# Where an attention pair's step yields: before its masks, or behind its scores over global keys

## The chip, the cores and the metric

One core of one Trainium2 chip runs the whole program. Five engines work side by side, each through its own queue in order: PE (TensorE, matrix products, whose weight loads are listed as PEld), DVE (VectorE), ACT (ScalarE), POOL (GpSimd) and SP (SyncE, which here issues the transfers). The metric is the device time of one execution in microseconds; lower is better. Times of the kernel are medians over runs, and a profile is one execution taken by the hardware profiler.

## The reference

The program is a network of two blocks on x of shape (16, 512, 256): 16 sequences, 512 tokens, 256 channels. Each block adds a gated branch twice, after a layer norm with a modulation:

```python
h = _layernorm(x, axis=-1) * (1 + ca) + sa
x = x + ga * _L0_attn_ref(h, ...)      # recurrent "fast weights", chunks of 16 tokens
h = _layernorm(x, axis=-1) * (1 + cb) + sb
x = x + gb * _L0_ffn_ref(h, ...)       # low-rank: two products, Gelu, two products
...
x = x + ga * _L1_attn_ref(h, L1_attn_w_attn, L1_attn_w_proj)   # the part that is changed
...
x = x + gb * _L1_ffn_ref(h, ...)       # squared-relu channel mix with a sigmoid gate
```

The branch that the change touches is attention with 16 heads of 16 channels, over a window of 64 tokens and four global keys:

```python
i = np.arange(T)[:, None]
j = np.arange(T)[None, :]
causal = j <= i
local = causal & (j >= i - LOCAL_WINDOW + 1)
mask = local | g_row & causal | g_col & causal      # g_row, g_col: tokens 0 to 3
...
att = jnp.einsum('bhqd,bhkd->bhqk', q, k) * scale
att = jnp.where(mask, att, jnp.finfo(att.dtype).min)
att = jax.nn.softmax(att, axis=-1)
y = jnp.einsum('bhqk,bhkd->bhqd', att, v)
```

## The kernel before

**Units and streams.** The work is cut into 16 units u: half of the sequences (8 of 16) times 64 tokens, halves alternating. Each unit passes five streams, written as Python generators: `prepare` (projections, short convolution, spilled to DRAM), `chain` (the recurrence: two pieces of 32 tokens, each two chunks of 16; the two halves have separate chains that run at the same time), `mlp` (output projection of the recurrence, then the low-rank branch with its burst of eight Gelu), `attend` (the windowed attention) and `mix` (the channel mix). A stream runs up to its next `yield`, which is one step.

**What sets the order.** `timetable` (L1120) gives each step of a unit a due time by hand, for instance 24 for `attend`, the last 19 of them between u + 3.05 and u + 3.95; L1135 sorts all steps of all units by due time and writes them in that order. So instructions of one step stand together in program order, and between two steps of one stream stand steps of others. The tile framework then gives every instruction its place in its engine's queue when the kernel is built: of what it takes to be ready, the earliest written goes first (two bursts are raised by `high_priority`). Tiles with one tag share a fixed number of slots.

**PSUM.** Eight banks: one holds the recurrence's state (`fw`), three are shared by everybody under the tag `bank`, four under `abank`. An abank is asked for by `sc` (four at a time), `st` (four), `py` and `pz` (one each), and by `ph` of the Gelu burst.

**An attention pair.** `window_attention` (L769) treats the eight sequences of a unit as four pairs r. A pair has the steps

- `find_maxima(r)` (L877): scores `sc` with queries in rows, masks, a maximum on DVE (`mx`, L888); for far units (tb > 1) also scores `sg` over the global keys. POOL splits the maxima in three bf16 parts. It is run one pair ahead.
- `weigh(r)` (L904), first step: two dummy matmuls (`hold`, L194) and a transposition of the maxima into `pmx`, ACT copies it to `mxT` (L910), then scores `st` with keys in rows (L916) and the maxima subtracted by matmuls with `sel` (L920). The step ends there (L921).
- second step: four mask matmuls (L924, recorded at L869), four exponentials `pT` on ACT (L926); for far units scores `tg` over the global keys, two `hold` matmuls, the exponential `pg` (L938), and the global keys' part of `py` (values) and `pz` (sums); then the window's part of `py` (L957) and `pz` (L966). All products of `mm` are recorded at L872.
- third step: 1 / pz by Ln and Exp on ACT (`rs`, L976, L977), and `yT` on DVE (L981).

After each two pairs comes the projection `pproj` (L1003).

**Neighbours in the order.** Between the first and the second step of the pairs the due times put, in the middle of the kernel: a norm of `channel_mix` (transposes `pt_d`, L361, which eight ACT instructions `hp`, L367, read), its product `pka` (L1040, whose end ACT's `mix`, L1030, and `ka`, L1052, wait for), and `prepare`'s product `pp` (L441) with a norm `pt_c` of the next attention. The `ph` burst of a unit is written between the second and the third step of another unit's second pair. The recurrence's exponentials on ACT are L541 (`e_k`, `e_v`) and L612 (`hid`).

Of the kernel before, what the change touches and what calls it, by code (L numbers as in the profile page):

```python
# [95 lines left out]
def adaln_blocks(ctx: ExitStack, tc: tile.TileContext, a: dict, out: bass.AP):  # L96
# [14 lines left out]
    def bank(name):  # L111
        return ps.tile([P, 512], F32, tag="bank", name=name)

    def abank(name):
        return ps_a.tile([P, 512], F32, tag="abank", name=name)
# [4 lines left out]
    def t2k(stream, name, shape=None):  # L120
        return work.tile(shape or [P, 512], F32, tag=f"t2k_{stream}", name=name, bufs=RING[stream])
# [72 lines left out]
    def hold(dst, n):  # L194

        for _ in range(n):
            nc.tensor.matmul(
                dst, lhsT=ident, rhs=w_attn[:, 0, : dst.shape[1]], start=True, stop=True, skip_group_check=True
            )
# [569 lines left out]
    def window_attention(i, x):  # L769
# [4 lines left out]
        far, last = tb > 1, tb == T // TB - 1  # L774
# [88 lines left out]
        def window(r, k2, e):  # L863
            return keys[:, k2, r, 2 * e : 2 * e + 2].rearrange("p s t -> p (s t)")

        def add_mask(dst, query_first):
            at = 2 * min(tb, 2) + (0 if query_first else 6)
            m = masks[:, at : at + 2].unsqueeze(1).to_broadcast([P, 2, 2, P])
            nc.tensor.matmul(dst, lhsT=ident_bf, rhs=m, start=False, stop=True, skip_group_check=True)  # L869

        def mm(dst, lhsT, rhs, start=False):
            nc.tensor.matmul(dst, lhsT=lhsT, rhs=rhs, start=start, stop=False, skip_group_check=True)  # L872
# [31 lines left out]
        def weigh(r, outs):  # L904
            tag, q = f"{i}_{r}", queries(r)
            pt = bank(f"pmx{tag}")
            hold(pt[:, P:], 2)
            nc.tensor.matmul(pt[:, :P], lhsT=maxima[r % 2], rhs=ident_bf, start=True, stop=True)
            mxT = work.tile([P, P], BF16, tag="mxT", name=f"mxT{tag}", bufs=1)
            nc.scalar.copy(mxT, pt[:, :P])  # L910

            st = [abank(f"st{tag}_{j}") for j in range(4)]
            for s, k2, e in slots:
                for j in range(4):
                    rows = slice(32 * j, 32 * (j + 1))
                    mm(st[j][:, s * P : (s + 1) * P], window(r, k2, e)[rows], q(k2, e)[rows], s == 0)  # L916
            for s, k2, e in slots:
                for j in range(4):
                    rows = slice(32 * j, 32 * (j + 1))
                    mm(st[j][:, s * P : (s + 1) * P], sel[rows, s : s + 1].to_broadcast([32, P]), mxT[rows])  # L920
            yield  # L921
            pT = []
            for j in range(4):
                add_mask(st[j], False)  # L924
                pT.append(t2k("c", f"pT{tag}_{j}"))
                nc.scalar.activation(pT[j], st[j], AF.Exp)  # L926
            py, pz = abank(f"py{tag}"), abank(f"pz{tag}")
            if far:

                rg = slice(32 * r, 32 * (r + 1))  # L930
                tg = bank(f"tg{tag}")
                for s, k2, e in slots:
                    mm(tg[rg, e * P : (e + 1) * P], kglob[:, b0 + 2 * r + e, 16 * k2 : 16 * k2 + 32], q(k2, e), s == 0)
                for e in range(2):
                    mm(tg[rg, e * P : (e + 1) * P], selg[:, e], mxT)
                hold(tg[:, 2 * P :], 2)
                pg = work.tile([P, 2 * P], F32, tag="pg", name=f"pg{tag}", bufs=1)
                nc.scalar.activation(pg[rg], tg[rg, : 2 * P], AF.Exp)  # L938
                for s, k2, e in slots:
                    for j in range(4):  # L940
                        cols = slice(k2 * P + 32 * j, k2 * P + 32 * (j + 1))
                        mm(
                            py[32 * j : 32 * (j + 1), s * P : (s + 1) * P],
                            vglob[half][rg, e, cols],
                            pg[rg, e * P : (e + 1) * P],
                            s == 0,
                        )
                for k2 in range(2):
                    for j in range(4):
                        n = 4 * k2 + j  # L950
                        mm(
                            pz[32 * j : 32 * (j + 1), k2 * 2 * P : (k2 + 1) * 2 * P],
                            ones_g[rg, n : n + 1].to_broadcast([32, 32]),
                            pg[rg],
                            k2 == 0,
                        )
            for s, k2, e in slots:  # L957
                for j in range(4):
                    cols = slice(k2 * P + 32 * j, k2 * P + 32 * (j + 1))
                    mm(  # L960
                        py[32 * j : 32 * (j + 1), s * P : (s + 1) * P],
                        values[:, r, e, cols],
                        pT[j][:, s * P : (s + 1) * P],
                        s == 0 and not far,
                    )
            for s, k2, e in slots:  # L966
                for j in range(4):
                    mm(
                        pz[32 * j : 32 * (j + 1), s * P : (s + 1) * P],
                        ones,  # L970
                        pT[j][:, s * P : (s + 1) * P],
                        s == 0 and not far,
                    )
            yield
            rs = t2k("c", f"rs{tag}")
            nc.scalar.activation(rs, pz, AF.Ln)  # L976
            nc.scalar.activation(rs, rs, AF.Exp, scale=-1.0)  # L977
            yT = t2k("c", f"yT{tag}", [P, 2, 2, 2, WIN])
            halves = lambda t: t.rearrange("p (k e h t) -> p k e h t", k=2, e=2, h=2)
            for k2 in range(2):  # L980
                nc.vector.tensor_tensor(  # L981
                    yT[:, k2].rearrange("p h e t -> p e h t"), halves(py)[:, k2], halves(rs)[:, k2], mul
                )
            outs.append(yT)
# [4 lines left out]
        for b2 in range(NR // 2):  # L989
            gt = load_gate("c", 2, b0 + 4 * b2, f"c{i}_{b2}")  # L990
            outs = []
            for r in (2 * b2, 2 * b2 + 1):
                if r + 1 < NR:
                    find_maxima(r + 1)
                    yield
                yield from weigh(r, outs)
                yield
            po = bank(f"pproj{i}_{b2}")

            for n, yT in enumerate(outs):  # L1000
                for k2 in range(2):
                    for par in range(2):
                        nc.tensor.matmul(  # L1003
                            po[:, n * C : (n + 1) * C],
                            lhsT=yT[:, k2, par].rearrange("p e t -> p (e t)"),
                            rhs=w_proj[:, k2, par, :],
                            start=k2 == 0 and par == 0,
                            stop=k2 == 1 and par == 1,
                        )
            gated_residual("c", x, b2, po, gt, f"c{i}_{b2}")  # L1010
            yield
# [181 lines left out]
```

## Time and profile before

| | |
|---|---|
| time, median of 3 runs | 3243.3 us (3237.48 to 3245.96) |
| the profiled execution | 3245.84 us, its span 3244.0 us |
| granted TensorE clock, mean | 0.823 |
| busy in 1250 to 1400 us, of 150 | PE 130.92, DVE 126.50, ACT 89.52, POOL 88.48 |
| busy in 2920 to 3244 us, of 324 | PE 282.29, DVE 79.00, ACT 144.21, POOL 73.92 |
| longest waits of ACT | xp for pp 142.4, e_k for DVE 136.9, e_v for DVE 120.4, rs for pz 115.4 us |
| table loads on ACT | 103 at L224, 79 at L234, 15 at L541, 14 at L976, 10 at L977; 1283 ns each |

Busy time is the time in which an engine had an instruction running. The profile names a group of instructions by its line, engine and tiles (`py<-pT,values` is a product that writes py and reads pT and values). "31.1 <-ACT pT L926 30.2" behind such a group says that the engine stood idle for 31.1 us just before these instructions, and that 30.2 us of it ended when ACT's instruction at L926 finished. The chain of waits goes back from the last instruction, at each step to what released it; its shares say where the time lies that could not overlap. From about 2920 us on the recurrence has ended and only the last units' streams run.

### The profile page before, as it was taken

The numbers are of one execution on the slowest core, as the hardware profiler recorded it, in microseconds if no ns is written. First come the engines' busy times: TensorE is split into PE (matmuls) and PEld (weight loads), VectorE is DVE, ScalarE is ACT, GpSimd is POOL, SyncE is SP. The second block draws the span as 40 slices with busy tenths as digits, with TensorE's granted clock in tenths as the row PEclk, the third lists the DMA queues.
The fourth block names the chain that finished last, engine by engine and source line by source line (L and its number), as shares of the span: only waits on it lengthen the run. The fifth ranks groups of instructions, "written<-read, shape, count | busy, mean of one in ns | idle before, by whom it ended". The sixth has DMA issues, their size and how long they took to land.

```text
span 3244.0 us, 47232 instructions
## 1 busy us (share of the span) xinstructions
PE 2445.9 (75%) x17232; PEld 1472.7 (45%) x17232; DVE 2372.1 (73%) x4513; ACT 1762.4 (54%) x3738; POOL 1677.1 (52%) x1575
## 2 busy tenths in 40 slices
PE   3541156778787778988888888988888888889996
PEld 2110124444444445555455555554545555556564
DVE  1678787878868878878888888878878877873221
ACT  1652354555664656665665656565665545454543
POOL 0245555556656655655646565655556556553112
PEclk8775577878877887988889797989889787879898
DMA  5331112131403223130413122231404121112010
GB/s 150 75 69 20 46 34 70 31 73 39 97 17 77 62 57 76 48 85 21 103 30 94 45 68 65 51 83 34 99 14 105 28 70 37 57 39 59 17 28 27
DMA packets 439307, 186.46 MB, mean 57 GB/s; under 512 B 323937, under 2 KB 413090, under 8 KB 439074
## 3 DMA queue, kind: packets, MB, share of 16 engines
q1 hardware_dynamic: 439074, 183.44, 23.4%
q8 instruction: 135, 2.21, 0.3%
q14 instruction: 98, 0.80, 0.1%
HBM read 116.66 MB, written 66.72 MB: 57 GB/s over the span
## 4 chain that ended last, share of the span: by engine, by line
DVE 35%; POOL 22%; PE 21%; ACT 10%; issue 8%; DMA 3%; SPq 1%; POOLq 0%; DVEq 0%; ACTq 0%
POOL pd_o L533 6%; POOL pd_i L533 5%; DVE pd_kv L630 3%; DVE sc_v L526 3%; DVE pp L459 3%; DVE sv L527 3%; DVE mx L888 2%; DVE do L635 2%; PE st L872 2%; DVE di L635 2%; POOL pd_kv L533 2%; DVE scs L527 2%; PE pQ L742 1%; PE ph L735 1%; PE py L872 1%
## 5 line engine op out<-in xcount | busy, mean ns | idle before, releaser
L533 POOL TENSOR_TENSOR pd_o<-e_k,dt_v 128x1024 f32<-128x1024 f32 x128 | 299.4, 2346 | 242.0 <-DVE e_k L548 242.0
L533 POOL TENSOR_TENSOR pd_i<-e_v,dt_k 128x1024 f32<-128x1024 f32 x128 | 297.3, 2358 | 30.7 <-DVE e_v L548 30.7
L660 POOL TENSOR_TENSOR pd_kv<-hid,pd_kv 128x1024 f32<-128x1024 f32 x64 | 150.5, 2351 | 175.3 <-DVE fw L631 149.3
L872 PE MATMUL st<-qs,keys 32*128 32x128 f32 x2048 | 203.4, 321 | 46.2 <-DVE yT L981 23.3
L635 DVE TENSOR_REDUCE di<-pd_i 128x64 f32<-128x1024 f32 x128 | 155.6, 1216 | 108.6 <-POOL pd_i L533 108.6
L872 PEld LDWEIGHTS st<-qs,keys 32*128 32x128 f32 x2048 | 168.6, 211 | 122.0 <-DVE yT L981 34.3
L872 PE MATMUL sc<-keys,qs 32*128 32x128 f32 x2048 | 167.3, 327 | 74.1 <-DVE yT L981 47.9
L635 DVE TENSOR_REDUCE do<-pd_o 128x64 f32<-128x1024 f32 x126 | 152.9, 1215 | 91.2 <-POOL pd_o L533 91.2
L707 PE MATMUL pwo<-w_WoT,oT 128*128 128x256 f32 x256 | 107.0, 579 | 136.7 <-POOL oT L700 135.9
L872 PEld LDWEIGHTS sc<-keys,qs 32*128 32x128 f32 x2048 | 133.3, 215 | 141.0 <-DVE yT L981 51.2
L888 DVE TENSOR_REDUCE mx<-sc 128x4 f32<-128x512 f32 x256 | 168.0, 682 | 18.5 <-PE sc L869 18.3
L526 DVE TENSOR_TENSOR sc_k<-tok,fw 128x1024 f32<-128x1024 f32 x128 | 155.7, 1216 | 13.8 <-ACT tok L596 12.1
L533 POOL TENSOR_TENSOR pd_kv<-hid,dt_v 128x1024 f32<-128x1024 f32 x64 | 150.5, 2352 | 25.7 <-DVE hid L622 22.7
L630 DVE TENSOR_TENSOR_SCAN pd_kv<-within,pd_kv 128x1024 f32<-128x1024 bf16 x64 | 156.4, 2443 | 0.7
L526 DVE TENSOR_TENSOR sc_v<-tok,fw 128x1024 f32<-128x1024 f32 x128 | 151.0, 1216 | 1.5
L527 DVE TENSOR_REDUCE sv<-sc_v 128x64 f32<-128x1024 f32 x128 | 150.4, 1212 | 0.0
L981 DVE TENSOR_TENSOR yT<-py,rs 128x256 f32<-128x256 f32 x128 | 51.6, 417 | 131.2 <-ACT rs L977 130.8
L735 PE MATMUL ph<-PT,w_v 64*128 64x512 f32 x256 | 119.7, 725 | 34.9 <-ACT z L224 19.8
L707 PEld LDWEIGHTS pwo<-w_WoT,oT 128*128 128x128 f32 x256 | 69.3, 289 | 163.1 <-POOL oT L700 150.3
L1003 PE MATMUL pproj<-w_proj,yT 128*128 128x256 f32 x512 | 129.8, 395 | 17.1 <-DVE yT L981 12.6
L926 ACT ACTIVATE pT<-st 128x512 f32<-128x512 f32 x256 | 133.6, 619 | 15.7 <-PE st L869 15.6
L454 ACT COPY xp<-pp 128x512 f32<-128x512 f32 x96 | 56.6, 589 | 156.8 <-PE pp L441 142.4
(248 smaller groups left out, 7039.2 us busy)
## 6 DMA issues: line engine op xcount, KB each, us to landing
values<-values SPq DMA_DIRECT2D x56, 256.0 KB
gate_a<-gates SPq DMA_DIRECT2D x64, 128.0 KB
xa<-in_x_dram SPq DMA_DIRECT2D x32, 256.0 KB
x<-in_x_dram SPq DMA_DIRECT2D x32, 256.0 KB
gate_c<-gates SPq DMA_DIRECT2D x64, 128.0 KB
gate_d<-gates SPq DMA_DIRECT2D x64, 128.0 KB
q<-y SPq DMA_DIRECT2D x64, 128.0 KB
dt_q<-q SPq DMA_DIRECT2D x32, 256.0 KB
```

The costliest lines, as they stand in the source:

```text
L526: engine.tensor_tensor(pr, tok.unsqueeze(1).to_broadcast(every), w.unsqueeze(2).to_broadcast(every), mul)
L527: nc.vector.tensor_reduce(dst, pr, AX.X, add)
L533: engine.tensor_tensor(pr, hid.unsqueeze(2).to_broadcast(every), tok.unsqueeze(1).to_broadcast(every), mul)
L630: nc.vector.tensor_tensor_scan(flat, within, flat, 0.0, mul, add)
L635: nc.vector.tensor_reduce(t, pr, AX.X, add)
L660: nc.gpsimd.tensor_tensor(po, qh.unsqueeze(2).to_broadcast([P, R, D, CH]), upto, mul)
L707: nc.tensor.matmul(po[:, n * C : (n + 1) * C], lhsT=pair(oT, k, 2 * b2 + n), rhs=w_o[:, k, :], start=k == 0, stop=k == 1,)
L735: nc.tensor.matmul(ph, lhsT=w_v1[rows, f // 2, :], rhs=pT[rows], start=True, stop=True)
L872: nc.tensor.matmul(dst, lhsT=lhsT, rhs=rhs, start=start, stop=False, skip_group_check=True)
L888: nc.vector.tensor_reduce(mx[:, j], sc[j].rearrange("p (s k) -> p s k", s=NS), AX.X, ALU.max)
L926: nc.scalar.activation(pT[j], st[j], AF.Exp)
L1003: nc.tensor.matmul(po[:, n * C : (n + 1) * C], lhsT=yT[:, k2, par].rearrange("p e t -> p (e t)"), rhs=w_proj[:, k2, par, :], start=k2 == 0 ...
```

## The change

The `yield` between the first and the second step of `weigh` moves down: from behind the subtraction of the maxima to behind the exponential `pg` of the scores over the global keys (for near units, behind the four `pT`). The first step now ends with all exponentials written, and the second has the products with values and ones alone; the tiles `py` and `pz` are asked for behind the yield. The number of steps and all due times stay, and so does every instruction.

```diff
@@ -918,13 +918,11 @@
                 for j in range(4):
                     rows = slice(32 * j, 32 * (j + 1))
                     mm(st[j][:, s * P : (s + 1) * P], sel[rows, s : s + 1].to_broadcast([32, P]), mxT[rows])
-            yield
             pT = []
             for j in range(4):
                 add_mask(st[j], False)
                 pT.append(t2k("c", f"pT{tag}_{j}"))
                 nc.scalar.activation(pT[j], st[j], AF.Exp)
-            py, pz = abank(f"py{tag}"), abank(f"pz{tag}")
             if far:
 
                 rg = slice(32 * r, 32 * (r + 1))
@@ -936,6 +934,9 @@
                 hold(tg[:, 2 * P :], 2)
                 pg = work.tile([P, 2 * P], F32, tag="pg", name=f"pg{tag}", bufs=1)
                 nc.scalar.activation(pg[rg], tg[rg, : 2 * P], AF.Exp)
+            yield
+            py, pz = abank(f"py{tag}"), abank(f"pz{tag}")
+            if far:
                 for s, k2, e in slots:
                     for j in range(4):
                         cols = slice(k2 * P + 32 * j, k2 * P + 32 * (j + 1))
```

## The prediction

> **What bounds the kernel now.** I read the page's busy table first, then its chain, then the groups of the one pair step, then the order of time around two such steps.
>
> ```profile
> PE 2445.9 (75%) x17232; PEld 1472.7 (45%) x17232; DVE 2372.1 (73%) x4513; ACT 1762.4 (54%) x3738; POOL 1677.1 (52%) x1575
> PEclk8775577878877887988889797989889787879898
> DVE 35%; POOL 22%; PE 21%; ACT 10%; issue 8%; DMA 3%; SPq 1%; POOLq 0%; DVEq 0%; ACTq 0%
> ```
>
> No engine is full. The chain that ended last is the recurrence's for more than half (DVE 35%, POOL 22%); PE has 21% of it. In the windows view of 1250 to 2750 DVE is busy 120 to 126 of every 150 us, PE 124 to 130. Which of the two paces the middle? The copies to PT (L725, one for each unit) start at 1482, 1666, 1847, 2028, 2209 and 2391 us: a unit takes 181 to 184 us, although the granted clock of these windows moves between 0.84 and 0.91. So the middle hardly follows PE's speed. The last 324 us are different: there PE is busy 282.29, DVE 79.00, and the chain's largest lines are PE's.
>
> Now the step that is changed. The groups view gives what its matmuls waited for:
>
> ```profile
> L926 ACT ACTIVATE pT<-st 128x512 f32<-128x512 f32 x256 | 133.6, 619 | 15.7 <-PE st L869 15.6
> L872 PE MATMUL py<-pT,values 128*32 128x128 f32 x2048 | 110.5, 322 | 31.1 <-ACT pT L926 30.2
> L872 PE MATMUL py<-pg,vglob 32*32 32x128 f32 x1536 | 55.1, 283 | 38.7 <-ACT pg L938 38.7
> ```
>
> Over the kernel PE stands 30.2 + 38.7 = 68.9 us between its scores and its values, because the exponentials come between them. That is all that this change can take from PE. Two pair steps of one unit, in order of time (start, duration, engine, line; in brackets the idle time before it and who ended it):
>
> ```profile
> 1448.59 0.66 PE L361 MATMUL pt_d<-blocks,xn_d 128*128 128x128 f32 x4
> 1449.08 1.03 PE L869 MATMUL st<-masks,ident_bf 128*128 128x512 bf16 x4
> 1449.28 2.48 ACT L367 ACTIVATE hp<-pt_d,mod 128x64 f32<-128x64 f32 x8 [1.83 <-PE pt_d L361]
> 1451.61 2.10 ACT L926 ACTIVATE pT<-st 128x512 f32<-128x512 f32 x4
> 1453.93 1.44 PE L872 MATMUL py<-pg,vglob 32*32 32x128 f32 x32 [1.66 <-ACT pg L938]
> ...
> 1486.48 3.70 PE L1040 MATMUL pka<-mix,w_W_kT 128*128 128x512 f32 x8
> 1490.02 1.03 PE L869 MATMUL st<-masks,ident_bf 128*128 128x512 bf16 x4
> 1490.22 1.33 ACT L1030 ACTIVATE mix<-hp,mu 128x512 f32<-128x512 f32 x2 [5.24 <-PE pka L1040]
> 1491.46 2.04 ACT L926 ACTIVATE pT<-st 128x512 f32<-128x512 f32 x4
> 1493.95 1.07 PE L872 MATMUL py<-pg,vglob 32*32 32x128 f32 x32 [0.74 <-ACT pg L938]
> ```
>
> The other streams' work (pt_d, pka) stands before the masks, where nothing has to be waited for, and behind the masks PE waits. The four pairs of a unit have these waits before py: 1.66 (pt_d ahead of the masks), 0.74 (pka ahead), 0.46 (nothing of others near), 0.18 us (pp and pt_c); 3.04 together, and they repeat almost to the hundredth from unit 5 to unit 10.
>
> **The change part by part.** No instruction, transfer or wait is added or removed. The four masks, the four pT exponentials, and in a far unit tg's scores, its two hold matmuls and the pg exponential are written one step earlier, ahead of what other streams write between the two steps. The moved part issues nothing on DVE, POOL or SP and no DMA, so those queues keep their own order; what it is moved past on PE and ACT is pt_d/hp, pka/mix, pp and pt_c/hTc. abanks are asked for in the same order as before (st four, py and pz, then ph), and ph started right behind pz's first matmuls in every far unit, so I expect the ph burst to stay there.
>
> First, the waits. First pair: the masks come at pt_d's old place, 1448.6; the masks and tg take 3.2 us of PE (1449.08 to 1452.27), so they end at 1451.8; pT is no longer behind hp (2.48 us) and ends near 1451.1, pg near 1452.2, while PE does pt_d (0.66). The 1.66 goes. Second: pka (3.70) covers the exponentials; 0.74 goes. Third: nothing stands there to be put between; 0.46 stays. Fourth: pp covers; 0.18 goes. So 2.58 of 3.04 us, 85%; of 68.9 us that is 58 us of PE time.
>
> Second, what of it is on the path. Around 1448 the chain runs through POOL pd_o, DVE do and off_b, not through PE: the first pair's wait is hidden behind the recurrence there, and costs only where that cover is gone, in the tail. Around 1486 it runs through pka, mix, pT, pg, py, ph: the second pair's wait is on it. Second pairs from the first unit on wait 0.07, 1.04, 1.04, 1.05, nine times 0.74, then 1.71 and 1.79: 3.2 + 6.7 + 3.5 = 13.4 us. In the tail unit 14's first pair waits 4.02 us, and there the chain does go through hp and pT (2.36 and 1.95 us from 3011.07); I take 4.0. Gain: 17.4 us. The bounds are 7 us (the waits in the tail alone: pg 8.5 us from 2920 on, 85% of it) and 68.9 us (all).
>
> Third, what it costs. pt_d and pka start 3.2 us later, and their readers with them: hp, mix, ka. In the second pair ACT is without a gap from 1490.22 to the table load at 1496.95 that opens the Gelu burst. With pT and pg done by 1490.2, mix waits for pka until 1493.4 and ends at 1494.7, where mix, pT and pg together ended at 1493.9: the burst opens 0.8 us later, if the tok copies behind it stay behind it; 0 if they go first. I take 0.4, for 16 units 6 us (0 to 13). hp, 3 us later in the first pair, is followed by steps that wait long anyway (mixture, pka a unit's fifth later); nothing in the middle, at most 3 us where the tail has no cover. tg takes one of the three banks 3 us before pt_d or pka do, and gives it back as much earlier; nothing.
>
> Sum: 3245.84 (the profiled execution: span 3244.0 and 1.8 around it) - 17.4 + 6 = 3234.4. The median of the runs shown is 2.5 us below that execution, so 3232 in its terms, 0.35% faster.
>
> The clock I leave where it is. The row: from 1495.50 to 1502.30 the granted clock is 0.50 while PE is busy in all 6.80 us, and 1.00 in the 13.70 us before, with 12.96 busy. The Trainium skill ("TensorE: Matmul & The Clock Gate", What's actually happening) says that half rate follows an idle window of about 3.4 us and full rate a busy one; by it no wait of 0.2 to 1.7 us costs clock, and closing them brings none, so the sum stays. The row does not obey it cleanly, so the clock is an open term of either sign, which the unit lengths above bound: 3 us in 181 at most between 0.84 and 0.91.
>
> A rule against the change: the same page (Architectural detail: the array is 16× 32×32) says that ACT is a strict FIFO while PE may pull weight loads ahead. This trace agrees in kind: ACT stood 5.24 us at mix. By it, each of the delayed readers would hold up all of ACT, which is the second rival.
>
> **The rivals.** One: the waits go, and the time doesn't (or the order on PE comes out as it was). For it: the unit length that ignores the clock, and 22% of the chain on POOL; against it: the chain through the second pair. Time 3243, or 3236 if the tail's 7 us are kept.
>
> Two, slower: ACT's queue. Three of a unit's four pairs put ACT work of others (hp, mix, xp or hTc) behind PE work that now starts 3.2 us later. If such an instruction stands in ACT ahead of an exponential of the recurrence (e_k, e_v L541, hid L612), DVE and then POOL start late, and that chain is 57% of the path. One such meeting for each unit is 16 x 3.2 = 51 us; two halves alternate, so I count half: 26 us, time 3269. It decides once DVE's waits for these exponentials, now 18.8 + 5.8 + 20.4 = 45 us, pass some 60, since the gain is only 11. For it: ACT is 54% busy and in order, and the wait of ACT for pka is 76.2 us already. Against it: total ACT work is unchanged, and pT and pg move out of the same queue's later part.
>
> **How the numbers follow.** Forecast (waits go, partly on the path): 0.50, its own range 3205 to 3243. Hidden or not done: 0.12. Slower by ACT's queue: 0.38, from 3250 to 3295 (51 us, all of it, at the end). A change under 0.3%, 10 us, is what a measurement here can't tell from none. The forecast gives 0.42 faster and 0.08 same, the first rival 0.11 same and 0.01 faster, the second 0.37 slower and 0.01 same: 0.43, 0.20, 0.37. For 8 in 10 the range leaves out the gains over 43 us, which need waits removed that are hidden now, and the upper end of the second rival: 3200 to 3285.
>
> **What would show it.** Right: PE's idle time before py falls from 68.9 to about 10 us; between the last sel and the masks PE has no other stream's work, and pt_d, pka and pp stand between the hold matmuls and py; pT starts ahead of hp; the unit length stays 180 to 182. Wrong: py still waits on pg; ph enters before pz, or the burst's table loads (103 + 79 + 15 + 14 + 10) change in number; the wait of ACT for pka grows past 76.2 by more than 16 us; DVE's waits for e_k, e_v and hid pass 60; or the unit length moves by over 2 us, which would say that the order of the recurrence itself was changed by what was thought to be beside it.

## The result: 2.9% slower

The changed kernel takes 3339.27 us (median of 4 runs, 3338.53 to 3340.08), the kernel before beside it 3240.77 (4 runs): ratio 1.0292, 95% interval 1.0279 to 1.0306, 98.5 us more. The prediction, 3232 us in a range of 3200 to 3285, was wrong. These lines of the changed kernel's profile answer to those shown of the kernel before: the busy table, the granted clock in 40 slices, the chain by engine.

```profile
PE 2432.6 (73%) x17232; PEld 1492.8 (45%) x17232; DVE 2386.1 (71%) x4513; ACT 1771.8 (53%) x3738; POOL 1673.6 (50%) x1575
PEclk8775676878787879778888788888878887879998
PE 26%; DVE 19%; POOL 10%; ACT 7%; issue 5%; DMA 1%; SPq 0%; POOLq 0%; ACTq 0%; DVEq 0%
```

PE, DVE, ACT and POOL are busy for as long as before, within 15 us. So nothing was added; they wait more. The chain of the changed kernel is followed back to 1064 us only, so its shares add up to 68% and can't be laid beside those of before as they stand. Counted for both from 1502 to 2295 us, PE has 41% of it (21% before), DVE 29% (37%) and POOL 12% (23%): PE is ahead in the middle, where the recurrence was. The groups that changed (line, engine, tiles, count; busy us, mean ns; idle before them and who ended it):

```profile
L925 ACT ACTIVATE pT<-st 128x512 f32<-128x512 f32 x256 | 134.3, 603 | 88.6 <-PE st L869 88.6
L872 PE MATMUL py<-pT,values 128*32 128x128 f32 x2048 | 99.5, 311 | 18.4 <-ACT pT L925 17.7
L872 PE MATMUL py<-pg,vglob 32*32 32x128 f32 x1536 | 59.1, 297 | 29.4 <-ACT pg L936 29.1
L454 ACT COPY xp<-pp 128x512 f32<-128x512 f32 x96 | 56.4, 587 | 197.6 <-PE pp L441 183.5
L982 DVE TENSOR_TENSOR yT<-py,rs 128x256 f32<-128x256 f32 x128 | 50.5, 414 | 146.3 <-ACT rs L978 146.3
```

PE's wait ahead of py, which was to fall from 68.9 to about 10 us, is 17.7 + 29.1 = 46.8 us. pT stands early in ACT's queue, as foreseen, and there ACT waits for pT's masks: 88.6 us where it was 15.7. ACT's wait at xp, the entry of `prepare`, rose from 142.4 to 183.5 us.

The copies to PT, one for each unit, show where the time lies. Before they start at 1302, 1482, 1666, 1847, 2028, 2209, 2391 us, after at 1292, 1502, 1701, 1899, 2097, 2295, 2493. Until 1292 us the changed kernel is 10 us ahead; then one unit takes 210 us, and each that follows 198 in place of 181. The tail is as long as before (from the last PT 206 against 213 us). So the loss is in the far units of the middle, and it repeats.

One piece of a middle unit, in order of time (start, duration, engine, line; in brackets the wait):

```profile
1922.33 1.28 ACT L977 ACT_TABLE_LOAD   x1
1923.63 0.60 ACT L977 ACTIVATE rs<-pz 128x512 f32<-128x512 f32 x1
1924.24 1.28 ACT L224 ACT_TABLE_LOAD   x1
...
1928.90 1.09 ACT L224 ACTIVATE sg<-pr 128x512 f32<-128x512 f32 x2
1930.00 1.28 ACT L234 ACT_TABLE_LOAD   x1
1931.30 0.63 ACT L978 ACTIVATE rs<-rs 128x512 f32<-128x512 f32 x1
...
1931.96 0.76 DVE L982 TENSOR_TENSOR yT<-py,rs 128x256 f32<-128x256 f32 x2 [9.68 <-ACT rs L978]
```

The same instructions in the kernel before:

```profile
1869.56 0.60 ACT L976 ACTIVATE rs<-pz 128x512 f32<-128x512 f32 x1
...
1871.46 0.63 ACT L977 ACTIVATE rs<-rs 128x512 f32<-128x512 f32 x1
...
1872.13 0.76 DVE L981 TENSOR_TENSOR yT<-py,rs 128x256 f32<-128x256 f32 x2 [2.49 <-ACT rs L977]
```

The second pair's root, Ln and then Exp, stood within 1.9 us before, and DVE waited 2.49 us for it. Now the end of the Gelu burst and a Tanh burst with their table loads stand between the two, 7.7 us from start to start, and DVE, which has the recurrence behind it in its queue, stands for 9.68 us. Nothing in the change touches these instructions.

Over three middle units (from the eighth PT to the eleventh) DVE idles 31.0 us a unit before and 45.8 after, 14.8 of the 17 us. The two waits of DVE that grew most are this one at yT and one at `pp`, in `prepare`, for ACT's instruction on the same tile (0.6 us a unit before). In one unit, the first line before (1847.3 to 2028.2 us), the other two after (1899.3 to 2097.2; in all, times, longest):

```profile
DVE yT L981 <- ACT rs L977: 2.5, 1, 2.5
```

```profile
DVE yT L982 <- ACT rs L978: 9.9, 2, 9.7
DVE pp L459 <- ACT pp L457: 7.9, 2, 4.8
```

These two rose by as much as DVE's whole idle time; of the others some rose and some fell. At yT the lines above show the reason, ACT's new order. The wait at pp was not followed further.

### The profile page after: what moved, and what is told of

It reads as the page before. It is cut to its first block, busy times and chain, and to the rows that moved or that the text cites. A ratio compares the mean times of both kernels' runs of the same rounds, so it can differ in the third digit from the quotient of the medians.

```text
span 3337.4 us, 47259 instructions
## 1 busy us (share of the span) xinstructions
PE 2432.6 (73%) x17232; PEld 1492.8 (45%) x17232; DVE 2386.1 (71%) x4513; ACT 1771.8 (53%) x3738; POOL 1673.6 (50%) x1575
## 4 chain that ended last, share of the span: by engine, by line
PE 26%; DVE 19%; POOL 10%; ACT 7%; issue 5%; DMA 1%; SPq 0%; POOLq 0%; ACTq 0%; DVEq 0%
POOL pd_i L533 3%; DVE sv L527 2%; DVE sc_v L526 2%; PE st L872 2%; DVE pd_kv L630 2%; PE pQ L742 2%; PE ph L735 2%; PE pp L441 2%; PE pr L1061 2%; POOL pd_o L533 2%; PE pproj L1004 1%; PE pka L1041 1%; DVE pp L459 1%; PE sc L872 1%; PE pkv L1078 1%
## 5 line engine op out<-in xcount | busy, mean ns | idle before, releaser
L872 PE MATMUL sc<-keys,qs 32*128 32x128 f32 x2048 | 185.6, 321 | 80.3 <-DVE mx L888 73.9
L872 PEld LDWEIGHTS st<-qs,keys 32*128 32x128 f32 x2048 | 176.9, 223 | 126.3 <-DVE mx L888 47.0
L872 PEld LDWEIGHTS sc<-keys,qs 32*128 32x128 f32 x2048 | 155.4, 214 | 135.4 <-DVE mx L888 88.3
L707 PE MATMUL pwo<-w_WoT,oT 128*128 128x256 f32 x256 | 99.4, 553 | 149.6 <-POOL oT L700 134.2
L925 ACT ACTIVATE pT<-st 128x512 f32<-128x512 f32 x256 | 134.3, 603 | 88.6 <-PE st L869 88.6
L630 DVE TENSOR_TENSOR_SCAN pd_kv<-within,pd_kv 128x1024 f32<-128x1024 bf16 x64 | 174.7, 2730 | 0.6
L454 ACT COPY xp<-pp 128x512 f32<-128x512 f32 x96 | 56.4, 587 | 197.6 <-PE pp L441 183.5
L982 DVE TENSOR_TENSOR yT<-py,rs 128x256 f32<-128x256 f32 x128 | 50.5, 414 | 146.3 <-ACT rs L978 146.3
L1004 PE MATMUL pproj<-w_proj,yT 128*128 128x256 f32 x512 | 122.7, 386 | 12.5 <-DVE yT L982 10.5
```

The lines of the kernel that those rows point to most:

```text
L630: nc.vector.tensor_tensor_scan(flat, within, flat, 0.0, mul, add)
L707: nc.tensor.matmul(po[:, n * C : (n + 1) * C], lhsT=pair(oT, k, 2 * b2 + n), rhs=w_o[:, k, :], start=k == 0, stop=k == 1,)
L1004: nc.tensor.matmul(po[:, n * C : (n + 1) * C], lhsT=yT[:, k2, par].rearrange("p e t -> p (e t)"), rhs=w_proj[:, k2, par, :], start=k2 == 0 ...
```

## The experiments

Five theories were told apart. A: the root's two halves were parted. B: tg asks for one of three shared banks a step earlier. C: the moved work itself holds up PE's and ACT's queues. D: the order of all engines, made when the kernel is built, came out anew, and the new one is worse. E: PE's longer waits cost twice, by the clock that falls behind them. All times stand against runs of the kernel before on the same chip. "Unit" is the mean of three PT distances in the middle; "moved rows" counts, from the traces, the fewest of the 4513 rows of DVE's queue that must move to turn the order of the kernel before into that of the run (rows with the same tiles and shape are taken in order).

| run | time, us | ratio (95% interval) | unit, us | moved rows of DVE |
|---|---|---|---|---|
| before | 3243.3 | | 181 | |
| after | 3339.27 | 1.0292 (1.0279 to 1.0306) | 198 | 1148 |
| e1 second pairs alone | 3263.95 | 1.0076 (1.0061 to 1.0091) | 184 | 705 |
| e2 all but second pairs | 3332.19 | 1.029 (1.0272 to 1.0309) | 195 | 1049 |
| e3 masks and pT alone | 3282.65 | 1.0138 (1.0119 to 1.0157) | 188 | 1139 |
| e4 after, root raised | 3297.25 | 1.0184 (1.0165 to 1.0203) | 188 | 1276 |
| e5 before, root raised | 3247.4 | 1.0004 (0.999 to 1.0017) | 181 | 448 |
| e6 bank request alone | 3243.41 | 0.9995 (0.9986 to 1.0004) | 181 | 0 |
| e7 first pairs alone | 3324.47 | 1.0236 (1.0206 to 1.0267) | 197 | 936 |
| e8 fourth pairs alone | 3340.56 | 1.0287 (1.0264 to 1.0309) | 194 | 1085 |
| e9 49 pairs, queues held | 3284.43 | 1.0124 (1.0107 to 1.0141) | 188 | 0 |
| e10 same pairs, order free | 3310.87 | 1.0201 (1.0182 to 1.0219) | 194 | 1075 |
| e11 after, DVE and POOL as before | 3298.44 | 1.0168 (1.0153 to 1.0183) | 191 | 0 |
| e12 before, DVE and POOL as after | 3469.78 | 1.069 (1.0672 to 1.0708) | 209 | 1148 |
| e13 as e9, pT ahead of mix | 3270.38 | 1.0075 (1.0062 to 1.0088) | 184 | 0 |
| e14 after, waits filled | 3459.09 | 1.0656 (1.0643 to 1.067) | 201 | 1148 |
| e15 as e13, second pairs alone | 3242.38 | 0.9996 (0.9987 to 1.0005) | 181 | 0 |
| e16 as e13, first pairs alone | 3261.61 | 1.005 (1.0036 to 1.0063) | 183 | 0 |
| e17 due times shifted | 3279.21 | 1.0108 (1.0092 to 1.0123) | 186 | 886 |
| e18 after, waits filled less | 3339.47 | 1.0292 (1.0279 to 1.0306) | 198 | 1148 |

No version beats the kernel before.

### Parts of the change, order free: e1 to e4

e1 and e2 divide the change by pairs; the yield stands at its new place for some pairs and at the old for the rest. This is e1; e2 has `r != 1` in both conditions:

```diff
-            yield
+            if not (r == 1):
+                yield
...
+            if r == 1:
+                yield
             py, pz = abank(f"py{tag}"), abank(f"pz{tag}")
```

e3 puts the yield between the pT exponentials and `py, pz`, so that tg, its hold matmuls and pg stay behind it. e4 is the changed kernel with this edit:

```diff
-            nc.scalar.activation(rs, pz, AF.Ln)
-            nc.scalar.activation(rs, rs, AF.Exp, scale=-1.0)
+            with tc.high_priority():
+                nc.scalar.activation(rs, pz, AF.Ln)
+                nc.scalar.activation(rs, rs, AF.Exp, scale=-1.0)
```

> The yield stands at its new place for a unit's second pair (r == 1) alone, at the old one for the other three. Theory A (the roots parted): in the changed kernel the second pair's Ln of pz stands in the Gelu burst and its Exp behind that burst and the Tanh burst, 7.1 us after it, and DVE stands 9.7 us at yT in place of 2.5; 7.2 us for each of the six units that are 17 us longer, 43 us of the 98.5 lost. In this kernel's order the Exp is behind one Gelu and a table load, with no Tanh burst, so A expects yT's wait near 3 to 5 us, and 3240 to 3275 us. Theory B (the bank): tg asks for one of the three shared banks one step earlier, so pka or pp wait for it; here only pka is behind tg, so B expects a third of the loss, 3260 to 3280. Theory C (the other pairs do it: hp, pp and hTc behind pT in ACT's queue): near 3241.

> The other way round: new place for the first, third and fourth pair, old place for the second. A: in the middle units the second pair's Exp is only one copy behind its Ln, DVE does not stand at yT for long (under 3 us), so 3240 to 3290: what is left is what A does not explain. B: tg is ahead of pt_d, pp and pt_c, two thirds of the loss or more, 3305 to 3339. C: all of it, 3325 to 3340.

> Masks and pT are ahead of the yield in all four pairs, tg's scores, the hold matmuls and pg behind it with the values, so tg asks for its bank where it did before. B: the loss goes, 3235 to 3265. A: in this order the second pair's Exp stands behind five Gelu and two table loads, though not behind the Tanh burst, so yT still waits for some 6 to 8 us and 3290 to 3330. C: pT is as early as in the changed kernel, 3320 to 3340.

> The changed kernel with Ln and Exp of the roots (L976, L977 of before) raised to the front by the planner's priority, in all pairs: the second pair's Exp is then behind one Gelu and two table loads. A: yT's wait falls from 9.7 to some 3 to 5 us, and the time to 3270 to 3300 if only the direct 43 us come back, to 3240 if the rest followed from it. B and C: nothing of theirs is touched, 3325 to 3345.

Measured: 23, 92, 42 and 57 us slower than before. By the bounds that were set, e1 agrees with A and B, e2 with B and C, e3 with none of the three. The parts do not add: 23 and 92 make 115, and the whole is 98.5. e4 won back 42 us, as much as theory A asked for, and in its middle units DVE no longer waits at yT for ACT's root (0.0 us a unit in place of 9.9, the unit 188 in place of 198), while the wait at pp stays (8.8). But its order of DVE also differs from the changed kernel's in 925 rows, so that some of the 42 may be due to these. That left a loss which no single place held.

### Root and bank in the kernel before, single pairs: e5 to e8

e5 is e4's edit in the kernel before. e6 moves one line there, `tg = bank(f"tg{tag}")`, ahead of the old yield. e7 and e8 are e1's edit with `r == 0` and `r == 3`.

> The kernel before (all values behind the old yield), with only the two activations of the softmax's root (Ln and Exp to rs) raised in the order that is made at build. Nothing is left out. Theory A (in the changed kernel the loss of about 42 us comes from a root whose two halves were parted by the Gelu burst): before, the two halves stand 1.3 us apart, so nothing is to be mended; DVE waits only 2.5 us a unit at yT. By A the time is 3215 to 3245 (at best 16 x 1.7 us gained, at worst nothing). If raising the root is good by itself, whatever the place of the scores, e4's 42 us was no repair of the change's own damage and this run gains as much: about 3200.

> The kernel before, with only the request of tg's bank moved ahead of the yield; its matmuls, the masks and both exponentials stay behind it. Nothing is left out. Theory B (the three shared banks are handed out in the order of the requests, and tg asks one step earlier, ahead of pt_d, pka and pp, so a bank is held across the step and others' matmuls wait): the loss that went with tg's place (57 us, e3 against the change) appears here without any work moved, 3270 to 3300. Theory C (what costs is work: exponentials and matmuls ahead of other streams' in PE's and ACT's queues): no work has moved, 3241 within 10.

> The change for the first pair of each unit alone (pt_d/hp stand between its scores and values). Nothing is left out. The prediction: nothing in the middle, 3 to 4 us gained in the tail: 3237 to 3244. Theory B: one of three pairs with work of others behind tg, about a third of 57 us: 3255 to 3265. Theory C: hp behind pT and pg in ACT's queue, 3 us later for 16 units: up to 48 us, 3250 to 3290. Theory A has no part here (its root is the second pair's): the wait at yT stays at 2.5 us a unit.

> The change for the fourth pair of each unit alone (pp, pt_c, hTc stand between its scores and values). Nothing is left out. The prediction: 0.18 us a unit of wait goes, 3241 within 5. Theory B: tg's bank comes ahead of pp, which is the mixer's own input path (xp): a third to a half of 57 us, 3260 to 3275, with PE waiting at pp or pt_c for a bank. Theory C: xp and hTc late in ACT's queue, ACT's wait at xp for pp grows from 11.7 us a unit towards 20; 3250 to 3290. If pairs 0 and 3 each add up to little, the loss of e2 (91 us) is no sum over pairs.

e5 is the kernel before to 0.04%, so a raised root is no gain by itself. In e6 the build gave every engine the very order of the kernel before, so it says nothing against a bank that is held longer; it shows that the request's place remade nothing and cost nothing. e7 and e8 ended the sum by pairs: one pair in four costs 79 us, another 95, alone nearly what all four do together. No theory of a price at each place expects that.

What these slow kernels have in common is the last column of the table. The change issues nothing on DVE, and 1148 of DVE's 4513 rows stand elsewhere; of POOL's 1575 it is 339. Where no row moved (e6), no time moved. The count is no measure of the loss, though: in e5 448 rows moved and no time did, and e4 has more moved rows than the changed kernel and is faster.

### Queues held: e9 to e13, e15 and e16

The next kernels are built twice. The first build, of the kernel before, only gives its queues; in the second they are imposed by edges that order instructions without a wait:

```diff
+    for queue in order or []:
+        queue = [by_key[k] for k in queue]
+        for one, two in zip(queue, queue[1:]):
+            tc.add_manual_dep(
+                two, one.name, mybir.DependencyInfo(mybir.DependencyClass.NoSync, mybir.DependencyReason.DATA), reason="order"
+            )
```

In the traces of e9, e11, e13, e15 and e16 no row of DVE's or POOL's queue has another place than in the kernel before, and e15, as fast as that kernel, suggests that the edges by themselves cost nothing that can be seen. In e9 just the change's own instructions are then moved (PE's directly behind the last `sel` matmul, ACT's pT and pg ahead of the readers of what they passed):

```diff
+        pe[:] = rest[: a + 1] + mine + rest[a + 1 :]
...
+        hit = [n for n in range(max(0, p - 40), p) if reads(at[act[n]]) & late]
```

This could be done for 49 of the 64 pairs; for the other 15, nine of them the fourth pairs of units 4 to 12, the yield stays at its old place. That held queues and early scores would wait for each other there is not shown by a run.

> Every engine's queue is held in the order of the kernel before (DVE, POOL and SP to the last instruction), and only the change's own instructions are moved in PE's and ACT's queues: masks, tg's scores and hold matmuls directly behind the last sel matmul, pT and pg ahead of the readers of the work that they passed. That is what the prediction took the change to be. 49 of the 64 pairs are moved (all third pairs, 14 of 16 first ones, 12 second ones, 7 fourth ones); the other 15 stay as before. Nothing is left out. Theory D (the order of all engines is made anew at the build when one yield moves, and the loss is in the new order): the loss is gone, 3222 to 3245. Theory C (the moved work itself holds up PE's and ACT's queues): a large part of the loss stays, 3280 or more.

> The same 49 pairs divided at the new place as in e9, but the order of all engines left to the build. Nothing is left out. Theory D: as slow as the change, 3300 to 3345, so that the difference to e9 is the new order alone. If it comes out near 3241, the 15 pairs left out were the harmful ones, and e9 says nothing on the order.

> The change in full (64 pairs), with DVE's and POOL's queues held in the order of the kernel before; PE's, ACT's and SP's orders are left to the build. Nothing is left out. Theory D in its narrow form (the recurrence's order on DVE and POOL is what was lost): 3230 to 3260. If the new order of PE and ACT is what costs, or the moved work, it stays above 3290.

> The reverse: the program of the kernel before (old yield), with DVE's and POOL's queues held in the order that the changed kernel has; PE's, ACT's and SP's orders are left to the build. Nothing is left out. Theory D in its narrow form: the change's slowness comes without the change, 3300 to 3345. If the order of DVE and POOL is a mere consequence, 3241 within 20.

e9 was to decide between C and D. At 39 us slower it misses D's bound (3222 to 3245) and lies just inside C's (3280 or more), though most of the 98.5 us are gone. As its queues are those of the kernel before but for the moved instructions, its trace can be laid beside it instruction by instruction. The plainest difference is at one place of each unit, here in order of time:

```profile
1671.74 1.13 PE L197 MATMUL tg<-w_w_attnT,blocks 128*128 128x256 f32 x4
...
1672.71 3.60 PE L1046 MATMUL pka<-mix,w_W_kT 128*128 128x512 f32 x8
...
1676.35 1.33 ACT L1036 ACTIVATE mix<-hp,mu 128x512 f32<-128x512 f32 x2 [8.18 <-PE pka L1046]
...
1677.59 2.03 ACT L928 ACTIVATE pT<-st 128x512 f32<-128x512 f32 x4
...
1679.63 0.37 ACT L939 ACTIVATE pg<-tg 32x256 f32<-32x256 f32 x1
...
1680.06 1.93 PE L872 MATMUL py<-pg,vglob 32*32 32x128 f32 x32 [3.75 <-ACT pg L939]
```

pT was left behind mix, which does not read pka and so was not passed by the rule above, but waits for pka all the same. ACT stands 8.18 us (5.24 before), PE then 3.75 (0.74 before). The windows view (us; PE, PEld, DVE, ACT, POOL busy; granted clock) shows what follows:

```profile
1672.00:1676.30 4.30, 4.30 (x12) 1.94 (x11) 2.42 (x3) 0.00 (x0) 4.30 (x3) 1.00 0.00 0
1676.30:1680.00 3.70, 0.01 (x1) 0.00 (x0) 3.70 (x7) 3.64 (x7) 1.07 (x1) 0.80 0.01 2
1680.00:1692.90 12.90, 12.07 (x79) 4.75 (x79) 5.98 (x14) 9.30 (x16) 4.37 (x3) 0.50 0.01 1
```

The burst runs at half clock (0.50), the e_k behind it comes late, and DVE waits 6.45 us for it (at 1692.43): its waits for e_k, e_v and hid are 46.5 + 4.8 + 10.0 = 61 us over the kernel (45 before). This is the mechanism of the prediction's second rival, over its bound of 60 us, but made by e9's own order of ACT's queue. In e13 pT and pg stand ahead of everything of the streams that they passed, mix included. e15 and e16 are e13 for one pair of four (12 second ones, 14 first ones).

```diff
-        hit = [n for n in range(max(0, p - 40), p) if reads(at[act[n]]) & late]
+        copied = max(n for n in range(p) if act[n][0] == first[0])
+        whose = {k[0] for k in passed} - {first[0]}
+        hit = [n for n in range(copied + 1, p) if act[n][0] in whose]
```

> As e9 (49 pairs, every queue in the order of the kernel before but for the change's own instructions), and in ACT's queue pT and pg also stand ahead of the work of the streams whose matmuls they passed, mix among it (in e9 they stood behind mix, which waited for pka). Nothing is left out. Theory D (the moved work is harmless, the remade order costs): the wait of 3.75 us at py and the half clock behind it go, the unit is 179 to 182 us, the time 3220 to 3248. Theory C (work moved ahead of the others' costs by itself): a unit stays at 185 us or more, 3265 or more.

> As e13, but for the second pairs alone (12 of 16), where the prediction put 13.4 us of its gain of 17.4 (10.1 for these 12 by the same waits) and 6 us of its cost. Nothing is left out. The prediction: 3232 to 3242. Theory C: 3255 or more, and then the second pair is the place.

> As e13, for the first pairs alone (14 of 16; pt_d and hp come behind their masks, pT and pg), every other queue held. Nothing is left out. The prediction: nothing in the middle, up to 3 us of cost and 4 of gain in the tail: 3238 to 3246. If the first pairs carry the loss of e13 against e15 (28 us), 3262 to 3275, a unit of 184 us, with PE waiting some 3 us at pt_b and DVE some 3 us at off_b.

e13: 25 us slower, inside C's bound (3265 or more), with a unit of 184, between D's 182 and C's 185: in the old order the moved work is not harmless. e15, the second pairs: no change (0.9987 to 1.0005). e16, the first pairs: 17 us slower. The third and fourth pairs were not run by themselves with held queues. For e15 the groups view names the two waits in question; the fence after it has the second of them in the kernel before:

```profile
L872 PE MATMUL py<-pg,vglob 32*32 32x128 f32 x1536 | 55.3, 283 | 30.0 <-ACT pg L939 30.0
L735 PE MATMUL ph<-PT,w_v 64*128 64x512 f32 x256 | 123.1, 741 | 43.4 <-ACT z L224 33.2 <-ACT PT L725 7.8 <-DVE yT L987 1.1
```

```profile
L735 PE MATMUL ph<-PT,w_v 64*128 64x512 f32 x256 | 119.7, 725 | 34.9 <-ACT z L224 19.8 <-ACT PT L725 7.7 <-DVE yT L981 3.4
```

PE's waits ahead of py fell by 12.5 us (68.9 to 30.0 + 26.4), and its waits for the burst's z rose by 13.4 (19.8 to 33.2). In the middle py starts 0.9 us earlier, counted from the last sel matmul (7.5 us to 6.6), and the table load of the burst 0.46 us later (10.47 to 10.93).

For e16 POOL's own order of time shows the loss; first the kernel before, then e16, at the same place of a unit:

```profile
1813.19 2.33 POOL L533 TENSOR_TENSOR pd_o<-e_k,dt_v 128x1024 f32<-128x1024 f32 x1 [0.45 <-DVE e_k L548]
1815.94 0.19 POOL L1026 COPY hlast<-hp 128x8 f32<-128x8 f32 x1 [0.42 <-ACT hp L367]
...
1817.35 1.04 POOL L351 TENSOR_TENSOR rs_b<-rs_b,mhalf 128x4 f32<-128x4 f32 x1
1818.36 2.35 POOL L533 TENSOR_TENSOR pd_kv<-hid,dt_v 128x1024 f32<-128x1024 f32 x1
```

```profile
1824.28 2.35 POOL L533 TENSOR_TENSOR pd_o<-e_k,dt_v 128x1024 f32<-128x1024 f32 x1
1828.46 0.19 POOL L1032 COPY hlast<-hp 128x8 f32<-128x8 f32 x1 [1.82 <-ACT hp L367]
...
1829.52 1.04 POOL L351 TENSOR_TENSOR rs_b<-rs_b,mhalf 128x4 f32<-128x4 f32 x1
1830.53 2.32 POOL L533 TENSOR_TENSOR pd_kv<-hid,dt_v 128x1024 f32<-128x1024 f32 x1
```

`channel_mix` keeps the last column of hp for the next unit by two small copies on POOL (`hlast`). They stand in POOL's queue between two products of the recurrence, pd_o and pd_kv. With pt_d behind the masks and tg, hp comes later, hlast waits 1.82 us in place of 0.42 (in six of the eight middle units 2.89 to 3.39), and everything of POOL's stands behind it: rs_b, for which DVE waits at off_b, and pd_kv. DVE's wait at off_b is the plainest sign, first before, then in e16:

```profile
L353 DVE SCALAR_TENSOR_TENSOR off_b<-mv_b,rs_b 128x4 f32<-128x4 f32 x16 | 19.7, 1231 | 12.0 <-POOL rs_b L351 12.0
```

```profile
L353 DVE SCALAR_TENSOR_TENSOR off_b<-mv_b,rs_b 128x4 f32<-128x4 f32 x16 | 19.5, 1220 | 28.7 <-POOL rs_b L351 28.7
```

That is 16.7 us more. e16's median is as much slower than its runs of the kernel before, and its profiled execution 19 us longer than the one profiled before, so this wait is of the size of the loss, and no closer agreement should be read into it. Two engines that the move does not touch carry its price here.

Against the same 49 pairs with a free order (e10, 65 us slower, as D expected), e13 leaves 40 us for the remade order, and e9, with pT at another place, 26. e11 holds DVE and POOL alone and gets back 46 of the 98 us, but stays above 3290, where D's narrow form (the order of DVE and POOL alone) expected 3230 to 3260. e12 forces the changed kernel's orders of DVE and POOL on the old program and is worse than both, far outside 3300 to 3345. So the narrow form falls twice; that the orders of the engines must fit each other agrees with both runs, and which rows do the harm is not shown.

### Due times shifted, without the change: e17

```diff
-        yield attend, [(2, u + 2.65, u + 2.8), (3, u + 2.95, u + 3.05), (19, u + 3.05, u + 3.95)]
+        yield attend, [(2, u + 2.65, u + 2.8), (3, u + 2.95, u + 3.05), (19, u + 3.06, u + 3.96)]
```

> The kernel before (old yield), with the due times of attention's last 19 steps 0.01 of a unit later (3.06 to 3.96 in place of 3.05 to 3.95), and the order of all engines left to the build, which remakes it: 1629 of DVE's 4474 rows stand elsewhere, against 2141 in the changed kernel. Nothing is left out. Theory D, general form (the order of before is a good one among many, and any remaking loses some per cent): 3265 to 3340. If only the divided step makes a bad order: 3241 within 15.

The counts in this expectation are nearly twice those of the table (886 and 1148), as a row that moved is counted where it left and where it came. The shift costs 34 us, inside D's bound. It is not a remade order alone, however: by the due times 53 steps of other streams, some four in each middle unit and pka's among them, are now written ahead of an attention step that they followed. No run holds the queues with these steps moved, so the two aren't told apart. And e5 speaks against the general form: its order was remade too, in 448 of DVE's rows, and nothing was lost, unless its raised root made up for it. So a near neighbour of the order before can be worse by 34 us, or as good.

### The clock: e14 and e18

Both are the changed kernel in its own queues, with dummy matmuls (`hold`) ahead of PE's waits for data. This is e14; e18 has 7, 3 and 1 of them at `pt` in units 6 to 12 and 2 at `py` in units 5 to 11:

```diff
             pt = bank(f"pt_{tag}_{r2}")
+            fill_wait(pt, {"a": (14, 0), "b": (8, 2)}.get(tag[0], (0, 0))[r2])
...
             py, pz = abank(f"py{tag}"), abank(f"pz{tag}")
+            fill_wait(py, 4 if far and r == 2 else 0)
```

> The changed kernel, every queue in its own order, with matmuls of no use in three of PE's waits that are for data: 14 of 128x512 ahead of the first pt_a of a unit (wait 10.6 us), 8 and 2 ahead of pt_b (5.3 and 2.2), 4 ahead of the third pair's py (3.4). Their results are overwritten; nothing is left out. Theory E (a longer wait of PE costs twice, as the granted clock is 0.5 for some 7 to 17 us behind it; in the middle the changed kernel spends 66 us of a unit at half clock, the kernel before 49): the half clock falls by 20 us a unit or more, the unit from 198 to 194 or less, the time below 3310. If the half clock stands where PE waits anyhow, 3339 within 10.

> As e14 with half the filling, in the middle units alone: 7 of 128x512 ahead of the first pt_a (some 6.5 us of the 10.6 by e14, where one took 0.93 us), 3 and 1 ahead of pt_b, 2 ahead of the third pair's py. Their results are overwritten; nothing is left out. Theory E (the half clock behind PE's long waits is on the path): the half clock falls from 66 to 50 us a unit and the unit from 198 to 194 or less, 3315 or less. If the clock is a consequence that costs nothing: half clock down, unit 198, 3339 within 8.

e14 filled more than the waits were (28 records of 0.64 us ahead of pt_a, and at the early units, where PE did not wait), so its 3459 us says nothing on E. e18 did: the half clock fell from 66 to 60 us a unit (windows view in steps of 1 us), less than was expected, and the mean granted clock of the profile rose from 0.813 to 0.826; a unit stayed at 198 us and the time at 3339.47. So where the filled waits stand, the lower clock cost nothing that can be seen, and E falls for these places. The other 11 of the 17 us of half clock that the changed kernel has more of in a unit (66 against 49) were not taken away, and what they cost is open.

## Why the prediction was wrong, step by step

**The step that failed** is a sentence in "The change part by part": "The moved part issues nothing on DVE, POOL or SP and no DMA, so those queues keep their own order". The first half is right; the second does not follow. The order of all queues is made at the build from one list, and by the traces 1148 of DVE's 4513 rows, 339 of POOL's 1575 and 898 of ACT's 3516 (without table loads) stood elsewhere afterwards. The prediction put the price of that at nothing. For the same 49 pairs, held queues cost 25 us (39 with pT placed as in e9) and a free order 65 (e13, e9, e10), so 26 to 40 us go with the order. Of the 98 us, 33 more came with the 15 pairs that weren't held (e10 to after); how much of these is the move and how much the order stays open. Nor are the 25 us a part of the 98 as they stand: they are the price of the move in the old order, and in the new one DVE loses its time elsewhere, at yT and pp.

**"hp, 3 us later in the first pair ... nothing in the middle"** failed too. hp's readers were given as the mixture and pka, a fifth of a unit later. The first reader is hlast, on POOL, in the recurrence's queue: 16.7 us (e16). In the changed kernel itself this sign is not there (DVE's wait at off_b is 9.5 us), as hlast has another place in the new order.

**The second pairs' 13.4 us**: the term was right as a wait and wrong as a gain. With held queues PE's waits ahead of py fall by 12.5 us, where 10.1 was expected for these 12 pairs, the burst opens 0.46 us later where 0.4 was taken, and nothing is gained (e15), since PE then waits for the burst's z. The chain was followed through py and ph; what set the pace there, by this reading, was ACT's queue up to the Gelu.

**PE's waits before py** (1.66, 0.74 and 0.18 us were to go, the third pair's 0.46 to stay) went where they were to go and grew where one was to stay: in the middle units the four pairs of the changed kernel wait 0.03, 0.00, 3.44 and 0.00 us, 3.47 in place of 3.04. The third pair, for which "nothing stands there to be put between", now has a burst of `prepare` with its two table loads between pT and pg in ACT's queue; the last line is the same wait before:

```profile
1961.85 2.07 ACT L925 ACTIVATE pT<-st 128x512 f32<-128x512 f32 x4 [1.36 <-PE st L869]
...
1963.93 1.28 ACT L224 ACT_TABLE_LOAD   x1
...
1965.23 1.09 ACT L224 ACTIVATE y<-pp 128x512 f32<-128x512 f32 x2
...
1966.33 1.28 ACT L234 ACT_TABLE_LOAD   x1
...
1967.63 0.38 ACT L936 ACTIVATE pg<-tg 32x256 f32<-32x256 f32 x1
...
1968.06 1.93 PE L872 MATMUL py<-pg,vglob 32*32 32x128 f32 x32 [3.44 <-ACT pg L936]
```

```profile
1912.64 1.08 PE L872 MATMUL py<-pg,vglob 32*32 32x128 f32 x32 [0.47 <-ACT pg L938]
```

Half of the 46.8 us that are left over the kernel is this wait in the middle units, and it comes from the remade order of ACT.

**tg's bank, "nothing"**: open. e3 leaves tg's part behind the yield and is 57 us faster than the whole change, but with a remade order of its own.

**The clock, left alone**: not shown to be wrong. The middle spends 66 us of a unit at half clock where it spent 49; taking away 6 of them changed nothing (e18), and the other 11 are untested.

**The rivals.** The second, slower by ACT's queue, had the sign, but by luck as far as its instructions go. Its mechanism is real (e9), and yet DVE's waits for e_k, e_v and hid, which were to pass 60 us, fell from 45 to 27. DVE does wait longer for ACT in the changed kernel, at pp (27.9 to 70.3 us), mix (37.4 to 62.0) and yT (130.8 to 146.3). ACT's order is new there, and whether the later start of pt_d and pka adds to it is not shown. The change was divided by pair and place, as if each had a price; e7 and e8 show that it hasn't. Of the signs that were to show the prediction wrong, the last was the right one: "the unit length moves by over 2 us, which would say that the order of the recurrence itself was changed by what was thought to be beside it". It moved by 17.

## What to carry to other kernels

Where a build makes the order of all queues from one list, an edit of one line can be an edit of every queue (e6 is one that wasn't): compare the built orders first, and allow for the remade order (here from nothing in e5 to 1.2% between e13 and e10, against the sum of the waits at stake, 2%) before any wait that the edit closes. To learn what a move itself is worth, hold the other queues and move it alone. For a step that is moved, follow every reader of every tile that it delays, small copies on other engines too: one that stood in front of a recurrence here went with a loss of 17 us (e16).

## What the runs showed of the hardware

The granted clock can fall in a shorter wait than expected. In e15 PE waits 2.09 us for the burst's z; the windows view before, over and behind it:

```profile
1864.00:1866.30 2.30, 2.27 (x36) 0.96 (x32) 2.20 (x5) 2.27 (x5) 0.55 (x1) 1.00 0.01 4
1866.30:1868.40 2.10, 0.04 (x1) 0.04 (x1) 2.07 (x2) 2.07 (x4) 1.49 (x2) 0.86 0.00 0
1868.40:1870.00 1.60, 1.60 (x4) 0.95 (x4) 1.53 (x4) 1.53 (x3) 0.00 (x0) 0.50 0.00 0
...
1874.00:1878.00 4.00, 4.00 (x41) 1.89 (x34) 0.66 (x1) 2.47 (x4) 2.34 (x2) 0.50 0.00 0
1878.00:1880.00 2.00, 2.00 (x7) 0.43 (x7) 1.38 (x3) 1.97 (x3) 0.00 (x0) 0.98 0.00 0
```

The clock fell some 0.6 us before the end of this wait (0.86 is the mean of 1.00 and 0.50 over 2.10 us), so behind 1.5 us without work, and stayed at 0.50 for about 10 us, with PE busy for nearly all of them. In the kernel before, PE waits 0.73 us there in this unit and the clock stays at 1.00:

```profile
1863.20:1864.00 0.80, 0.07 (x2) 0.04 (x1) 0.77 (x2) 0.79 (x3) 0.19 (x1) 1.00 0.00 0
```

The length of the wait doesn't decide it alone. One unit later in e15 an equal wait, 2.08 us, left the clock at 1.00; it fell only 2.4 us after the wait, for 3.5 us:

```profile
2047.60:2049.70 2.10, 0.02 (x2) 0.01 (x1) 2.00 (x4) 2.07 (x4) 1.52 (x2) 1.00 0.00 0
2049.70:2052.10 2.40, 1.87 (x5) 0.76 (x6) 2.33 (x4) 2.38 (x5) 0.00 (x0) 1.00 0.00 0
2052.10:2055.60 3.50, 3.50 (x38) 1.87 (x41) 2.86 (x9) 3.12 (x4) 2.12 (x1) 0.51 0.00 0
```

And the prediction's row, a fall at 1495.50 us with PE busy in 12.96 of the 13.70 us before, is near this place of an earlier unit in the kernel before. The Trainium skill ("TensorE: Matmul & The Clock Gate", What's actually happening) gives at least one idle window of about 3.4 us for the fall and at least one busy window of that length for the return; here the fall came in shorter waits or behind them, and the return after one such length or three. Nor is a lower clock a loss everywhere: e18 raised it in a few places and gained nothing.
